# Where softmax is divided: from the probabilities to the output of P @ latents, by a row of reciprocals sent through DRAM

## The chip, the cores and the metric

The kernel runs on one NeuronCore of a Trainium2 chip. A core has TensorE (matrix multiplication, called PE in the profile), VectorE (DVE), ScalarE (ACT), GpSimd (POOL) and SyncE (SP), which here issues all DMAs. The engines run side by side, each through its own list of instructions in order, and wait for each other by semaphores. On-chip data lies in SBUF with 128 partitions; matrix products land in PSUM. The metric is the device time of one execution in microseconds (us); the time of a kernel is the median of several runs.

## What is computed

One pre-norm transformer layer, eight sequences (batches) of 512 tokens, width 512: attention with low-rank queries and a shared latent for keys and values, then a gated feed-forward part with weights rounded to an 8-bit float format. Cut to the attention, where the change lies:

```python
q = rmsnorm(layernorm(x) @ wq_a.T, q_norm_w)                # 384 wide
q_nope, q_pe = split((q @ wq_b.T).reshape(b, s, 16, 192))   # 128 + 64 for each of 16 heads
kv_c, k_pe = split(layernorm(x) @ wkv_a.T)                  # latents 128, rotary key 64
kv_c = rmsnorm(kv_c, kv_norm_w)
k_nope, v = split((kv_c @ wkv_b.T).reshape(b, s, 16, 256))
scores = (q_nope @ k_nope.T + rope(q_pe) @ rope(k_pe).T) / sqrt(192)
attn = softmax(scores, axis=-1)                             # exp(s - max) / sum(exp(s - max))
x = x + (attn @ v).reshape(b, s, 2048) @ wo.T
x = x + ffn(layernorm(x))
```

The kernel folds weights: `wq_b` with the key half of `wkv_b` (tile `wa`), and the value half with `wo` (tile `wst`). Attention then works on the latents themselves: scores are `qn @ latents` plus the rotary part, and the output of a head is P @ latents (128 wide), multiplied by the folded output weights.

## The kernel before

The attention part is a list of 8 x 16 x 4 = 512 steps, one for each batch `b`, head `h` and tile `t` of 128 queries. `at(b, h, t)` is the number of a step. In each step the loop at the end of `attention` first calls `rest` of the step before, then `scores` of this one, and then whatever has been put into `work[i]` for this step, in the order in which it was put. All engines' instructions are recorded in this order (no scheduler moves them), so the position of a call decides where its instruction stands on its engine. In what follows i is the step `at(b, h, 3)` of a head's last tile.

- `scores` (L552): TensorE multiplies one query tile into a PSUM tile `sc` (four passes, L560 and L562). VectorE takes the negative maximum of each row (`nmax`, L564). ScalarE computes `pr` = exp(sc + nmax) with the sum of each row in `den` (L567).
- `rest` inside it (L569), called one step later: VectorE takes the reciprocal of `den` (L571), multiplies `pr` by it (L572), and transposes 32 x 32 blocks of it into `block` (L167, function `blocks`).
- `send` (L172), after every second tile: SP writes `block` (512 KB) to a DRAM tile `way` (L177), and after that has landed reads it back in four parts into `prT`, the transposed probabilities (L179). So transposition goes by way of DRAM.
- `attend` (L577), at step i+6: TensorE multiplies `prT` with the latents `kvt` into the PSUM tile `av` (8 passes, L583), and ScalarE copies `av` into `o`, a tile of the head with queries in the free dimension, and puts the queries back into order in doing so (L586).
- `sums` (L592), at i+7 for odd heads: GpSimd makes sums and differences of the two heads' halves of `o`, for a product by Strassen's method (seven products in place of eight).
- `output` (L606), for every fourth head: seven products of two pairs of heads with `wst` into the PSUM tiles `z_ps`, `u_ps`, `v_ps` (L628), each added to x by VectorE (L632). They are put at i+8 (`z_ps`, `u_ps`), i+12, i+15 and i+16. The odd head of the second pair gives its own `o` to `z_ps`, at step i+8.

`sc`, `av`, `qn_ps` and most other products take turns in one PSUM pool of six buffers (`ps_r`); `u_ps` and `v_ps` have a buffer of their own.

Between these calls lie others, at steps given by hand: projections of queries (`project`, `project_pe`), the latents of the next batch (`put_latents`), and in batches 1 to 6 the rounding of feed-forward weights (`round_piece`, with L71 to L82 on VectorE and L76, L77 on GpSimd). In batch 0 SP also loads the weights of all heads, and they are folded there (`fold_q`, `fold_o`).

`first` prepares the latents of batch 0. Its helper `normed` runs the moments of a tile, the standard deviation (ScalarE), its inverse, and then subtracts the mean.

The feed-forward part follows the attention and is not touched.

Of the kernel before, what the change touches and what calls it, by code (L numbers as in the profile page):

```python
# [35 lines left out]
F32 = mybir.dt.float32  # L36
F32R = mybir.dt.float32r
U32 = mybir.dt.uint32
AF = mybir.ActivationFunctionType
# [47 lines left out]
class Layer:  # L87
# [81 lines left out]
            x.rearrange("p (k c j) -> p k c j", c=NQ, j=Q),  # L169
        )  # L170

    def send(self, out, block):  # L172


        nc = self.nc
        way = self.dram.tile([NQ, Q, NQ, NT * 2 * Q], F32, tag="way", name="way", bufs=6)
        nc.sync.dma_start(way.rearrange("a j c x -> (a j) c x"), block.rearrange("p c k i -> p c (k i)"))  # L177
        for c in range(NQ):
            nc.sync.dma_start(  # L179
                out[c * Q : (c + 1) * Q].rearrange("j a k i -> j a (k i)"),  # L180
                way[:, :, c].rearrange("a j x -> j a x"),
            )

    def ffn_stats(self, x, small):

# [84 lines left out]
    def attention(self):  # L270
        tc, nc, ins, wp, xp = self.tc, self.nc, self.ins, self.wp, self.xp
        with ExitStack() as ctx:
# [279 lines left out]
            def scores(b, h, t, block):  # L552

                qn, qpe = state["qn", b, h], state["pe", b, h // 2]
                lat, _, kpe = state["latents", b]
                q = slice(t * P, (t + 1) * P)
                sc = ps_r.tile([P, S], F32, tag="r", name="sc")
                nc.tensor.matmul(sc, qn[:, q], lat[:, NR, :], start=True, stop=False)  # L560
                for part in range(2):
                    nc.tensor.matmul(sc, qpe[:, h % 2, q], kpe[:, part, :], start=False, stop=part == 1)  # L562
                nmax = sp.tile([P, 1], F32, tag="nmax", name="nmax")
                nc.vector.tensor_reduce(nmax, sc, AX.X, ALU.max, negate=True)  # L564
                pr = hp.tile([P, S], F32, tag="pr", name="pr")
                den = sp.tile([P, 1], F32, tag="den", name="den")
                nc.scalar.activation(pr, sc, AF.Exp, bias=nmax, accum_out=den)  # L567

                def rest():  # L569
                    rden = sp.tile([P, 1], F32, tag="rden", name="rden")  # L570
                    nc.vector.reciprocal(rden, den)  # L571
                    nc.vector.tensor_scalar(pr, pr, rden, None, ALU.mult)  # L572
                    self.blocks(block, pr, t)

                return rest

            def attend(b, h):  # L577
                prT = state.pop(("prT", b, h))
                del state["qn", b, h]
                kvt = state["latents", b][1]  # L580
                av = ps_r.tile([P, S], F32, tag="r", name="av")
                for kt in range(NT):
                    nc.tensor.matmul(av, kvt[:, kt, :], prT[:, :, :, kt, :], start=kt == 0, stop=kt == NT - 1)  # L583
                o = hp.tile([P, S], F32, tag="o", name="o", bufs=6)

                nc.scalar.copy(  # L586
                    o.rearrange("p (u t a i) -> p u t a i", u=2, t=2, i=Q),
                    av.rearrange("p (u a t i) -> p u t a i", u=2, t=2, i=Q),
                )
                state["o", b, h] = o  # L590

            def sums(b, h):  # L592

# [60 lines left out]
            def at(b, h, t=0):  # L654
                return (b * NH + h) * NT + t

            def put(i, f, *args):
                work[i].append(lambda: f(*args))
# [15 lines left out]
            def first():  # L674
                p, state["latents", 0] = latents(0)

                for _ in range(4):
                    pt = ps_r.tile([P, NC, P], F32, tag="r", name="warm")
                    for c in range(NC):
                        nc.tensor.transpose(pt[:, c, :], self.ident, self.ident)  # L680

                def normed(t):
                    p["moments"](t), p["deviation"](slice(t, t + 1)), p["deviation_inverse"](slice(t, t + 1))
                    p["center"](t)

                normed(0)
                p["transpose_x"](0)
                normed(1)
                for t in range(NT):
                    p["project_x"](t, (0,))  # L690
                    if t + 1 < NT:
                        p["transpose_x"](t + 1)
                    if t + 2 < NT:
                        normed(t + 2)
                    p["project_x"](t, (1,))
                p["norms"](), p["norms_inverse"]()
                for t in range(NT):
                    p["scale"](t)
                fold_q(0)
                p["rotary"]()  # L700
                for t in range(NT):
                    p["transpose_l"](t)
                rotate, hi, lo = project_pe(0, 0)
                p["rotary_parts"]()
                rotate()
                fold_q(1)
                project(0, 0)
                hi()
                project(0, 1)
                lo()  # L710
# [12 lines left out]
                    put_q(b, h)  # L723
            for b, h in ((b, h) for b in range(B) for h in range(1, NH, 2)):
                i = at(b, h, 3)
                put(i + 7, sums, b, h)
                if h % G == G - 1:

                    def projected(b=b, g=h // G, i=i):

                        late = (b, g) == (B - 1, NG - 2)
                        when = (8, 12, 17, 18, 19, 20) if late else (8, 12, 15, 16, 16, 18)
                        for n, f in zip(when, output(b, g)):
                            put(i + n, f)

                    put(i + 7, projected)

            for h in range(NH):
                if h >= 2:
# [78 lines left out]
            with tc.manual_schedule():  # L818
                first()
                load_q(2), load_q(3)  # L820
                prT = block = rest = None
                for i in range(len(steps) + 19):
                    if rest:
                        rest()
                        rest = None
                    if i < len(steps):
                        b, h, t = steps[i]
                        if t == 0:
                            prT = state["prT", b, h] = hp.tile(
                                [P, 2, NQ, NT, 2 * Q], F32, tag="prT", name="prT"  # L830
                            )
                        if t % 2 == 0:
                            block = hp.tile([P, NQ, NT, 2 * Q], F32, tag="block", name="block")
                        follow = scores(b, h, t, block)

                        def rest(follow=follow, block=block, prT=prT, t=t):
                            follow()
                            if t % 2:
                                self.send(prT[:, t // 2], block)

                    while work[i]:
                        work[i].pop(0)()
# [125 lines left out]
```

## Time and profile before

| | |
|---|---|
| median of 3 runs | 2741.95 us (2741.65 to 2743.36) |
| the profiled execution | 2745.5 us, of which 2743.7 are the span of the trace |
| TensorE busy | 2718.3 us (99%) |
| VectorE busy | 1884.3 us (69%) |
| ScalarE busy | 895.9 us (33%) |
| GpSimd busy | 597.6 us (22%) |
| DMA | 426 MB, 155 GB/s |

The span runs from the first to the last instruction of one execution. Busy times are sums of the instructions of an engine; a group of the profile is one line of the kernel on one engine with one operation and its tiles, with the count, the busy time, the mean duration of one (ns), and then the idle time of the engine just before, with what ended it. Attention takes the first 2230 us or so, the feed-forward part the rest.

### The profile page before, as it was taken

The page shows a single profiled execution, that of the slowest core. Times are in us where ns is not written, and L with a number is a line of the kernel's source. Part 1 is how long each engine was busy: PE and PEld are TensorE (multiplying, and loading weights), DVE is VectorE, ACT ScalarE, POOL GpSimd, SP SyncE. Part 2 cuts the span into 40 slices and gives each one's busy share as a digit, 9 for nine tenths or more (in the row PEclk, how much of TensorE's full clock was granted, in tenths as well). Part 3 has the DMA queues.
Part 4 walks back from the last instruction along what each step waited for, and adds up shares of the span by engine and source line. Part 5 has one row for each costly group of instructions (what it writes and reads, how often), then busy time and mean ns, then how long its engine had stood idle before and what let it go on. Part 6 is the DMA issues. An engine that isn't in the chain of part 4 may idle for free.

```text
span 2743.7 us, 29211 instructions
## 1 busy us (share of the span) xinstructions
PE 2718.3 (99%) x9280; PEld 1714.8 (62%) x9280; DVE 1884.3 (69%) x3683; ACT 895.9 (33%) x1958; POOL 597.6 (22%) x629
## 2 busy tenths in 40 slices
PE   9999999999999999999999999999999999999999
PEld 5465555555555555555555555555555578888887
DVE  5766787778777877787778777877777734333332
ACT  3333333333333333333333333333332333333332
POOL 1221222222222222122212221222111122222222
PEclk9999999999999999999999999999999999999999
DMA  3654465556555654565456445654565651111110
GB/s 125 207 189 160 167 203 171 157 168 202 169 159 173 201 165 155 171 214 159 154 182 203 159 154 177 208 162 152 183 203 168 201 188 62 66 63 64 66 62 20
DMA packets 262376, 426.07 MB, mean 155 GB/s; under 512 B 29648, under 2 KB 192592, under 8 KB 260688
## 3 DMA queue, kind: packets, MB, share of 16 engines
q1 hardware_dynamic: 262224, 424.21, 47.6%
q8 instruction: 74, 1.21, 0.2%
q14 instruction: 78, 0.64, 0.1%
HBM read 248.99 MB, written 175.11 MB: 155 GB/s over the span
## 4 chain that ended last, share of the span: by engine, by line
PE 90%; DVE 6%; ACT 2%; DMA 1%; issue 0%; SPq 0%; ACTq 0%; DVEq 0%
PE av L583 14%; PE sc L560 14%; PE qn_ps L548 10%; PE u_ps L628 7%; PE sc L562 7%; PE pu L261 6%; PE pd L893 6%; PE pg L261 6%; PE qpe_ps L516 6%; PE lr_ps L451 5%; PE v_ps L628 3%; PE z_ps L628 2%; DVE pr L572 1%; DVE block L167 1%; DVE nmax L564 1%; ACT pr L567 1%
## 5 line engine op out<-in xcount | busy, mean ns | idle before, releaser
L567 ACT ACTIVATE pr<-sc,nmax 128x512 f32<-128x512 f32 x512 | 351.8, 687 | 1294.9 <-DVE nmax L564 1289.1
L562 PE MATMUL sc<-kpe,qpe 128*128 128x512 f32 x1024 | 526.7, 595 | 0.0
L560 PE MATMUL sc<-lat,qn 128*128 128x512 f32 x1024 | 523.1, 592 | 0.0
L583 PE MATMUL av<-prT,kvt 128*128 128x512 f32 x1024 | 462.2, 594 | 3.1 <-DMA prT<-way 2.9
L564 DVE TENSOR_REDUCE nmax<-sc 128x1 f32<-128x512 f32 x512 | 338.5, 661 | 106.9 <-PE sc L562 106.6
L167 DVE STREAM_TRANSPOSE block<-pr 128x512 f32<-128x512 f32 x512 | 364.3, 711 | 27.5 <-DMA way<-block 10.0
L572 DVE TENSOR_SCALAR pr<-pr,rden 128x512 f32<-128x512 f32 x512 | 339.0, 662 | 18.1
L548 PE MATMUL qn_ps<-lat,wa 128*128 128x512 f32 x768 | 350.2, 592 | 0.0
L562 PEld LDWEIGHTS sc<-kpe,qpe 128*128 128x128 f32 x1024 | 194.6, 190 | 244.9 <-issue 242.0
L583 PEld LDWEIGHTS av<-prT,kvt 128*128 128x128 f32 x1024 | 194.3, 190 | 199.9 <-issue 189.0
L416 POOL TENSOR_TENSOR roped<-rope_own,rope_sw 128x512 f32<-128x512 f32 x72 | 91.3, 1268 | 909.4 <-DVE rden L571 822.7
L560 PEld LDWEIGHTS sc<-lat,qn 128*128 128x128 f32 x1024 | 188.8, 190 | 133.1 <-issue 108.8
L548 PEld LDWEIGHTS qn_ps<-lat,wa 128*128 128x128 f32 x768 | 145.2, 189 | 134.6 <-issue 122.6
L881 POOL TENSOR_TENSOR fl<-fuse,fh 128x512 fp32r<-128x512 f32 x96 | 126.1, 1315 | 383.3 <-ACT fh L880 383.3
L877 DVE SCALAR_TENSOR_TENSOR fuse<-pu,us,gate 128x512 f32<-128x512 f32 x96 | 72.0, 750 | 193.9 <-PE pu L261 190.9
L571 DVE RECIPROCAL rden<-den 128x1 f32<-128x1 f32 x512 | 81.3, 159 | 160.6 <-ACT pr L567 153.5
L76 POOL TENSOR_TENSOR q_r<-raw,q_m 128x256 f32<-128x256 f32 x72 | 66.2, 919 | 556.7 <-DVE q_m L74 371.1
L516 PE MATMUL qpe_ps<-lat,wqp 128*128 128x512 f32 x384 | 175.3, 592 | 0.7 <-issue 0.7
L261 PE MATMUL pu<-yh,wu 128*128 128x512 f32 x384 | 149.9, 390 | 0.0
L261 PE MATMUL pg<-yh,wg 128*128 128x512 f32 x384 | 149.7, 390 | 0.0
L893 PE MATMUL pd<-wd,fh 128*128 128x512 f32 x384 | 149.5, 389 | 0.0
L261 PE MATMUL pu<-yl,wu 128*128 128x512 f32 x384 | 149.4, 389 | 0.0
(116 smaller groups left out, 3688.8 us busy)
## 6 DMA issues: line engine op xcount, KB each, us to landing
way<-block SPq DMA_DIRECT2D x256, 512.0 KB, 2.8
prT<-way SPq DMA_DIRECT2D x1024, 128.0 KB, 2.8
wst<-wst_d SPq DMA_DIRECT2D x56, 512.0 KB, 4.4
wst<-wst_d SPq DMA_DIRECT2D x56, 384.0 KB, 3.9
x<-in_hid SPq DMA_DIRECT2D x60, 256.0 KB, 3.5
x<-x SPq DMA_DIRECT2D x16, 512.0 KB, 4.4
out<-o SPq DMA_DIRECT2D x32, 256.0 KB, 2.0
wst_d<-wst SPq DMA_DIRECT2D x8, 896.0 KB, 4.6
```

Source lines behind the costliest of these rows:

```text
L167: self.nc.vector.transpose(out[:, :, :, i : i + Q].rearrange("p c k i -> p k c i"), x.rearrange("p (k c j) -> p k c j", c=NQ, j=Q),)
L261: self.nc.tensor.matmul(ps, self.ffn_w[name, i][:, c * P : (c + 1) * P], y[k][:, c, :], start=c == 0 and k == 0, stop=c == NC - 1 and k == 1,)
L516: nc.tensor.matmul(ps, wqp_s[g][:, r, pj * P : (pj + 1) * P], lat[:, r, :], start=r == 0, stop=r == NR - 1)
L548: nc.tensor.matmul(ps, wa_s[g][:, j, r, :], lat[:, r, :], start=r == 0, stop=r == NR - 1)
L560: nc.tensor.matmul(sc, qn[:, q], lat[:, NR, :], start=True, stop=False)
L562: nc.tensor.matmul(sc, qpe[:, h % 2, q], kpe[:, part, :], start=False, stop=part == 1)
L564: nc.vector.tensor_reduce(nmax, sc, AX.X, ALU.max, negate=True)
L567: nc.scalar.activation(pr, sc, AF.Exp, bias=nmax, accum_out=den)
L572: nc.vector.tensor_scalar(pr, pr, rden, None, ALU.mult)
L583: nc.tensor.matmul(av, kvt[:, kt, :], prT[:, :, :, kt, :], start=kt == 0, stop=kt == NT - 1)
L628: nc.tensor.matmul(got[name][:, t, :], ops[p][left][:, t * P : (t + 1) * P], w[:, p, right, :], start=first and t == 0 and p == 0, stop=la ...
L893: nc.tensor.matmul(pd, f[:, i, t * P : (t + 1) * P], w["wd", i], start=i == 0 and f is fh, stop=i == NI - 1 and f is fl,)
```

## The change

The probabilities stay undivided. `den` becomes a tile of 128 x 4 for a head, and each tile's exp puts its sums into one column. After the last tile, VectorE takes the reciprocal of all four columns at once. P @ latents has the queries in its free dimension, so a divisor is wanted as a row that is the same on all partitions. It is made by two DMAs: one writes the 512 reciprocals to a DRAM tile in order of queries, the other reads them back as a row of 512 onto each of the 128 partitions, with a step of zero for the partition. `send` takes these two calls (`also`): it issues the first between the write to `way` and the four reads, and the second after the reads. `attend` no longer copies `av`; the multiplication of `av` by the row is put at the end of the list of the next step, i+7, on VectorE, in two halves, and writes `o`. `sums` and the call that places the products move from i+7 to i+8; the products stay at i+8 and after. Also, `first` now subtracts the mean before it takes the deviation, and a scratch size of the launch is set to 1024.

```diff
-    def send(self, out, block):
+    def send(self, out, block, also=()):
...
         nc.sync.dma_start(way.rearrange("a j c x -> (a j) c x"), block.rearrange("p c k i -> p c (k i)"))
+        for f in also[:1]:
+            f()
         for c in range(NQ):
             nc.sync.dma_start(
...
             )
+        for f in also[1:]:
+            f()
...
-                den = sp.tile([P, 1], F32, tag="den", name="den")
-                nc.scalar.activation(pr, sc, AF.Exp, bias=nmax, accum_out=den)
+                if t == 0:
+                    state["den", b, h] = sp.tile([P, NT], F32, tag="den", name="den")
+                den = state["den", b, h]
+                nc.scalar.activation(pr, sc, AF.Exp, bias=nmax, accum_out=den[:, t : t + 1])
 
                 def rest():
-                    rden = sp.tile([P, 1], F32, tag="rden", name="rden")
-                    nc.vector.reciprocal(rden, den)
-                    nc.vector.tensor_scalar(pr, pr, rden, None, ALU.mult)
                     self.blocks(block, pr, t)
+                    if t < NT - 1:
+                        return ()
+                    nc.vector.reciprocal(den, den)
+                    way = self.dram.tile([NT, P], F32, tag="den_way", name="den_way", bufs=3)
+                    row = state["den", b, h] = hp.tile([P, S], F32, tag="row", name="row")
+                    source = bass.AP(tensor=way.tensor, offset=way.offset, ap=[[0, P], [1, S]])
+                    return (
+                        lambda: nc.sync.dma_start(way.rearrange("t p -> p t"), den),
+                        lambda: nc.sync.dma_start(row, source),
+                    )
...
-                o = hp.tile([P, S], F32, tag="o", name="o", bufs=6)
-
-                nc.scalar.copy(
-                    o.rearrange("p (u t a i) -> p u t a i", u=2, t=2, i=Q),
-                    av.rearrange("p (u a t i) -> p u t a i", u=2, t=2, i=Q),
-                )
-                state["o", b, h] = o
+                row = state.pop(("den", b, h))
+
+                def normed():
+                    o = state["o", b, h] = hp.tile([P, S], F32, tag="o", name="o", bufs=6)
+
+                    to, by = (v.rearrange("p (u t a i) -> p u t a i", u=2, t=2, i=Q) for v in (o, row))
+                    of = av.rearrange("p (u a t i) -> p u t a i", u=2, t=2, i=Q)
+                    for u in range(2):
+                        nc.vector.tensor_tensor(to[:, u], of[:, u], by[:, u], ALU.mult)
+
+                put(at(b, h, 3) + 7, normed)
...
                 def normed(t):
-                    p["moments"](t), p["deviation"](slice(t, t + 1)), p["deviation_inverse"](slice(t, t + 1))
-                    p["center"](t)
+                    p["moments"](t), p["center"](t)
+                    p["deviation"](slice(t, t + 1)), p["deviation_inverse"](slice(t, t + 1))
...
-                put(i + 7, sums, b, h)
+                put(i + 8, sums, b, h)
...
-                    put(i + 7, projected)
+                    put(i + 8, projected)
...
-                            follow()
+                            also = follow()
                             if t % 2:
-                                self.send(prT[:, t // 2], block)
+                                self.send(prT[:, t // 2], block, also)
...
-    nc = bacc.Bacc("TRN2", target_bir_lowering=False, num_devices=1)
+    nc = bacc.Bacc("TRN2", target_bir_lowering=False, num_devices=1, dynamic_dma_scratch_size=1024)
```

## Prediction

> **What bounds the kernel now.** I read the page first, then the groups of TensorE by form, then the waits, and last the timeline at the places where TensorE stands idle. The page's engine line, its clock row and a VectorE group that goes:
>
> ```profile
> PE 2718.3 (99%) x9280; PEld 1714.8 (62%) x9280; DVE 1884.3 (69%) x3683; ACT 895.9 (33%) x1958; POOL 597.6 (22%) x629
> ...
> PEclk9999999999999999999999999999999999999999
> ...
> L572 DVE TENSOR_SCALAR pr<-pr,rden 128x512 f32<-128x512 f32 x512 | 339.0, 662 | 18.1
> ```
>
> TensorE is busy 99% at full clock, so nothing that another engine does less of is worth its busy time. Only a TensorE idle stretch that goes or comes counts. VectorE is at 69%, off the bound. How much is there to win? Starts of consecutive matmuls in the timeline keep a fixed pace (429 ns for a 512-column float32 pass, 216 for 256 columns). Adding up where a start comes later than that pace gives some 30 us in all: 9 us in the first 100 us, 6 us between 100 and 140 us, and about 2 us in each later batch of 271 us. The groups say who ends the later ones:
>
> ```profile
> L628 PE MATMUL u_ps<-wst,o 128*128 128x256 f32 x512 | 121.8, 381 | 5.9 <-DVE x L632 5.9
> ...
> L628 PE MATMUL z_ps<-wst,o 128*128 128x256 f32 x256 | 62.7, 382 | 5.2 <-ACT o L586 5.2
> ```
>
> After the second bar stands the idle time before: 5.9 us where `u_ps` waits until VectorE has drained it into x (L632), 5.2 us where `z_ps` waits for ScalarE's copy of o (L586). Counted by start to start the L632 wait is 0.95 us in each of batches 1 to 6 (the pair L562 starts at 380.60, the next matmul at 382.43: 1.83 us where 0.88 is usual) and 0.77 us twice in batch 7, 7.2 us in all. The `z_ps` wait is 0.82 us, once a batch.
>
> Now the normal `z_ps`, without a wait (h=3 of batch 1): the timeline of TensorE, then of VectorE (start, length, then engine and line):
>
> ```profile
> 407.24 1.03 PE L562 MATMUL sc<-kpe,qpe 128*128 128x512 f32 x2
> 408.11 1.02 PE L560 MATMUL sc<-lat,qn 128*128 128x512 f32 x2
> 408.57 1.03 PE L562 MATMUL sc<-kpe,qpe 128*128 128x512 f32 x2
> 409.43 1.89 PE L628 MATMUL z_ps<-wst,o 128*128 128x256 f32 x8
> ```
> ```profile
> 410.73 0.65 DVE L564 TENSOR_REDUCE nmax<-sc 128x1 f32<-128x512 f32 x1
> 411.30 0.42 DVE L81 SCALAR_TENSOR_TENSOR q_m<-q_r 128x256 f32<-128x256 f32 x1
> 411.76 0.83 DVE L82 SCALAR_TENSOR_TENSOR done<-q_m,q_r 128x256 fp32r<-128x256 f32 x1
> ```
>
> Call i the step of a head's last query tile. o of head h is made from av at step i+6; `z_ps` is multiplied at step i+8, after the scores of i+7 and i+8. Its first two passes use an older o; from 409.43 + 0.43 = 409.86 it needs the new one. ScalarE had made it at 408.1, 1.7 us early. The maximum of the scores of step i+7 (nmax, 410.73) comes *after* that time on VectorE: VectorE is 2.5 us behind the scores. This order is what the change meets. The one place in a batch where the copy is late (h=11; it runs from 552.21 to 552.78, held up by ScalarE's table loads and casts):
>
> ```profile
> 551.58 0.60 PE L628 MATMUL z_ps<-wst,o 128*128 128x256 f32 x2
> 552.84 1.56 PE L628 MATMUL z_ps<-wst,o 128*128 128x256 f32 x6 [0.66 <-ACT o L586]
> ```
>
> **The change part by part.** *Removed.* 512 reciprocals of 159 ns become 128, 512 multiplications of 662 ns (L572) go, 128 copies L586 of about 0.58 us leave ScalarE. VectorE gets 256 multiplications of 128x256 from PSUM. For these I have L252, the same shape but both operands in SBUF, at 549 ns, L81 (128x256, two float32 inputs) at 420 ns, and L632 with one operand in PSUM at 683 ns for twice the size, with starts 0.60 us apart in a row. I take 0.46 us, 0.36 to the start of the second; ends 0.42 and 0.55. VectorE: -512 x 0.662 - 384 x 0.159 + 256 x 0.46 = -282 us, to about 1600. All of it is hidden under TensorE. Its worth is what it does to the three waits.
>
> *The L632 wait goes.* In that stretch (369 to 382 us) VectorE saves two rows of L571 and three of L572 (0.5 to 1.5 us each), about 3 us; the draining that ended at 382.37 is needed at 381.6. Gain 7.2 us; between 0 and 7.2.
>
> *z_ps waits for VectorE instead of ScalarE.* The multiplication is put at i+7, at the end of that step's list, so on VectorE it stands behind nmax of i+7, and behind L81 and L82 where weights are rounded (batches 1 to 6). It can't start before the scores of i+7 are done: 407.24 + 1.03 = 408.27. With the relief VectorE is there in time. I followed its order from 401 us with the durations shown and the two removed rows left out: it reaches the qpe casts at 405.2, the block of i+6 at 407.0, and waits for the scores. From 408.30: nmax 0.57 to the next start, L81 0.46, L82 0.5 to 0.75, the first multiplication 0.46, and 0.06 to TensorE (as from the copy's end to the release above): 410.35 to 410.60 against 409.86. A new wait of 0.5 to 0.75 us; z_ps reads only the half that the first multiplication writes. Heads 3 and 7 of six batches: 12 x 0.6 = +7.2 us. Where no weights are rounded (h=15, batch 7, batch 0) the same sum without L81 and L82 ends 0.4 us before it is needed: no wait.
>
> At h=11 four more operations (L476, L479 twice, 0.53 us a pair) stand ahead, and ScalarE's chain of 5.51 us from one exp (546.02) to the next (551.53) stays, with its two table loads. It starts earlier by the removed rows: VectorE's block follows L415 at 542.94, nmax 543.8, exp 544.45 instead of 546.02, the next exp 549.96, block 550.7, nmax 551.35, L81 551.9, L82 552.4, L476 to L479 553.2, multiplication 554.25, TensorE at 554.8 instead of 552.84. That is 1.9 us more than the wait that is there, in six batches, and in batch 0, with a further 0.86 us of matmul ahead and no L81, 0.7: +12.1 us. Even with VectorE never late it would be 0.75 us each.
>
> *av keeps its PSUM buffer longer.* It is freed after nmax of i+7. The next user of the slot is a qn two steps later at the nearest; with a projection of 4 us between, it has 4 us to spare. At the other places three or more steps. Nothing. `sums` moves one step; its first reader is four steps on. Nothing.
>
> *Two more DMAs a head on SP.* den goes out (512 elements of 4 bytes) between way and the four prT loads, the row (256 KB) comes in behind them; the row waits on SP for den's landing, with the next head's weights and way queued behind it. In the steady state prT lands some 7 us before its av and SP spends 590 us waiting for VectorE's blocks: hidden. In batch 0 it isn't, since SP also loads weights there; between 60 and 165 us SP waits for a block under 2 us in all. Timelines of SP and TensorE, and a window row (its last three numbers are clock, DMA share, GB/s):
>
> ```profile
> 122.61 0.38 SPq L177 DMA_DIRECT2D way<-block  x1
> 128.60 1.75 SPq L179 DMA_DIRECT2D prT<-way  x4
> ```
> ```profile
> 132.79 5.37 PE L583 MATMUL av<-prT,kvt 128*128 128x512 f32 x8 [2.02 <-DMA prT<-way]
> ```
> ```profile
> 132.60:138.20 5.60, 5.41 (x9) 2.39 (x10) 5.24 (x13) 2.03 (x5) 2.95 (x4) 0.70 0.57 184
> ```
>
> Issue of way, landing 5.6 us later, four issues, landing 2.4 us later, and av starts with it. Slack before av is 4.2 us at head 1, 1.5 at head 2, none at 3 and 4, 6.8 at 5. Each head adds 0.43 us of issue (as the other rows) and 0.7 us of transfer ahead of the next way (at the start the 256 KB x loads, back to back, land 0.66 us apart: the issues at 8.56, 9.22 and 9.88 each wait for a landing); den's issue and landing lie under way's own landing. 1.1 us a head, less 0.5 of slack: head 3 is 2.8 us later, head 4 3.9 in all. The bounds for den: nothing at all, or, since no trace row has 512 packets in one DMA, prT held up behind it. Against this speaks the Trainium skill, DMA: Bandwidth & Descriptors, Rules for kernel authors: a non-contiguous last dimension becomes one descriptor for each element and should be rearranged. Nearest row: knw, 128 packets of 4 bytes, issues in 0.44 us. Four times that is 1.8 us, still under way's landing of 3 to 6 us. By the row +0, by the rule, if each engine's 32 writes take 0.1 us, 3 us a head and 12 in batch 0. I take the row and keep 12 for the range.
>
> The row also shows the clock at 0.70 after the 2.0 us wait: av took 5.37 instead of 3.60 us, 1.8 lost. The Trainium skill (TensorE: Matmul & The Clock Gate, Part 1) asks for a whole idle window of about 3.4 us before the clock halves; this trace did it with 2.0. By the rule a 2.8 us longer wait at head 3 (3.5 us in all) just does it, by the trace surely. +1.7. Batch 0: 3.9 + 1.7 = +5.6 us; between 0 and 17.
>
> *Start.* Centring moves ahead of the deviation, so it no longer waits for ScalarE's table load (1.28 us): xc at 4.5 instead of 6.24, the first transposes at 5.05 instead of 6.77. The weights' landing doesn't hold it (issued by 3.47, 4.9 us to land, the last quarter is needed after 10). -1.7 us; up to -3.4 if the clock also rises one window sooner. *End.* The last head's z_ps needs both multiplications (0.82 us) in place of one copy (0.57): +0.3. The scratch size setting issues nothing: 0.
>
> **Sum.** -7.2 + 7.2 + 12.1 + 5.6 - 1.7 + 0.3 = +16.3 us on the profiled span of 2743.7 (2745.5 with what lies around it). That execution was 3.6 us above the median of the runs; on the median 2741.95 it is 2758.3.
>
> **Rivals.** *The relief is all (faster).* If VectorE had the multiplication done within 1.58 us of the end of scores i+7, neither the old z_ps waits nor new ones are left: -7.2 - 6 x 0.82 - 1.7 = -13.8, 2728 us. For it: VectorE loses 15% of its work. Against it: nmax, L81 and L82 must come to under 1.1 us, and their rows come to 1.5 to 1.8. It decides where the multiplication stands in the order, not how busy VectorE is. *Small waits (no change).* z_ps waits at their least (12 x 0.45, 6 x 0.75), den and clock free, SP 1.2: -1.7 - 7.2 + 5.4 + 4.5 + 1.2 = +2.2, 2744 us. *den is slow.* The scatter holds up the queue by 3 us a head: batch 0 gives 17 instead of 5.6, 2770 us; only above 7 us a head would the later batches follow. That the change doesn't do what it says can't be: TensorE's and GpSimd's orders are the same in both, and the 512 L572 rows are gone.
>
> **How the numbers follow.** Main case 0.66, slow den 0.14, small waits 0.12, relief 0.08. A measurement of this kernel tells about 0.2% (5.5 us) from no change, so slower is 0.66 + 0.14 = 0.80, same 0.12, faster 0.08. The range runs from the small waits (2743) to a slow den with long z_ps waits (2774); outside lie the relief and a little at each end.
>
> **What would show it.** Right: z_ps with an idle time of 20 to 30 us ended by VectorE's o; u_ps<-o without its 5.9; av's wait for prT in batch 0 at 6 us or more; VectorE near 1600 us, ScalarE near 820; xc at 4.5. Wrong: z_ps idle under 8 us, prT landing no later at heads 3 and 4, waits of any other reader for the row, or a qn waiting for o.

## The result, and the profile after

The changed kernel takes 3462.3 us (median of 4 runs, 3459.7 to 3469.7) against 2742.7 beside it: a ratio of 1.2626 (95% interval 1.2603 to 1.2648), +720 us. The prediction was 2758.3 us with a range up to 2774. Slower was right; the size was wrong by a factor of 44.

All lines below are of the changed kernel's trace unless said otherwise; its line numbers are shifted (L597 is the av matmul, L646 the products, L606 the new multiplication, L181 prT's reads, L585 and L586 the writes of den and the read of the row). First the page's engine line and clock row, the av group, and VectorE's transposes, with the idle time before them and what ended it:

```profile
PE 2922.1 (84%) x9280; PEld 1769.2 (51%) x9280; DVE 1529.6 (44%) x3043; ACT 823.3 (24%) x1830; POOL 578.6 (17%) x629
...
PEclk9899999999999989998998899999998898999999
...
L597 PE MATMUL av<-prT,kvt 128*128 128x512 f32 x1024 | 632.0, 775 | 464.7 <-DMA prT<-way 254.5
L167 DVE STREAM_TRANSPOSE block<-pr 128x512 f32<-128x512 f32 x512 | 362.7, 708 | 1348.8 <-DMA way<-block 1291.1
```

The same two groups of the kernel before:

```profile
L583 PE MATMUL av<-prT,kvt 128*128 128x512 f32 x1024 | 462.2, 594 | 3.1 <-DMA prT<-way 2.9
...
L167 DVE STREAM_TRANSPOSE block<-pr 128x512 f32<-128x512 f32 x512 | 364.3, 711 | 27.5 <-DMA way<-block 10.0
```

TensorE is no longer busy 99% but 84%, and its clock row has eights in it (mean granted clock 0.929; 0.999 before). So the loss of 716 us in the span has two parts: 204 us more of busy time (2922.1 - 2718.3) and 513 us more of standing still. Of the 204 us, 170 are av's own passes (775 ns in the mean, 594 before), which run right behind the waits. Nearly all of the standing still is before av (464.7 us, 3.1 before), which waits for prT. The waits view puts 166 of these down to the row, which av doesn't read. In the trace the row landed after av had started in each of those cases, while every one of av's waits ended within 0.45 us of a landing of prT. VectorE's transposes wait 1348.8 us (27.5 before), because their `block` is still being written to `way`. The rows that this stands on are SP's: its DMAs with the median from issue to landing (us), and what SP waited for (total, times, longest):

```profile
way<-block SPq DMA_DIRECT2D x256, 512.0 KB, 6.9
...
den_way<-den SPq DMA_DIRECT2D x128, 2.0 KB, 10.7
```

```profile
SPq L181 <- DMA way<-block: 1766.5, 256, 12.2
...
SPq L586 <- DMA den_way<-den: 154.9, 62, 6.2
...
SPq L177 <- DVE block L167: 13.6, 17, 8.9
```

The same of the kernel before:

```profile
way<-block SPq DMA_DIRECT2D x256, 512.0 KB, 2.8
```

```profile
SPq L179 <- DMA way<-block: 779.6, 256, 5.8
SPq L177 <- DVE block L167: 589.6, 207, 10.5
```

SP's queue is what bounds the kernel now. Before, SP waited 780 us for `way` to land and had 590 us to spare waiting for blocks. After, it waits 1767 for `way` and 155 for den, and the wait for blocks is down to 13.6 us. The sum: 987 more for `way`, 155 for den, 256 more issues at 0.43 us (110), less the 576 of slack used up, is 676 of the 716 us. For a head that is 8.9 us more waiting where 4.6 were spare. One head in SP's timeline (start, length of the issue):

```profile
1004.37 0.38 SPq L177 DMA_DIRECT2D way<-block  x1
1004.84 0.43 SPq L585 DMA_DIRECT2D den_way<-den  x1
1014.33 1.74 SPq L181 DMA_DIRECT2D prT<-way  x4
```

`way` and den are issued at 1004.4 and 1004.8; prT's reads can't go out until `way` has landed, at 1014.3: ten microseconds, where `way` before took 2.6 at this step (9.6 is the median of the 128 such steps now). By the trace's packets, the last pieces of `way` and den are done by 1009.4, and then nothing moves until the landing. A window row (its last three numbers are clock, DMA share, GB/s):

```profile
1009.40:1014.30 4.90, 4.90 (x23) 3.79 (x22) 0.00 (x0) 0.00 (x0) 2.17 (x3) 1.00 0.00 0
```

The DMA engines have nothing left to move; what is late is the completion of the writes.

Last, the groups that the prediction looked at. They answer to the two that were shown of before:

```profile
L646 PE MATMUL u_ps<-wst,o 128*128 128x256 f32 x512 | 124.3, 387 | 4.2 <-DVE x L650 4.2
...
L646 PE MATMUL z_ps<-wst,o 128*128 128x256 f32 x256 | 67.7, 394 | 28.1 <-DVE o L606 27.6
```

`z_ps` waits 28 us for VectorE's multiplication (20 to 30 was forecast), `u_ps` 4.2 instead of 5.9. These were the right places, at 4% of the loss.

### The profile page after: what moved, and what is told of

Same layout as the page of the kernel before. It is cut to its first block, busy times and chain, and to the rows that moved or that the text cites. A ratio compares the mean times of both kernels' runs of the same rounds, so it can differ in the third digit from the quotient of the medians.

```text
span 3460.0 us, 29034 instructions
## 1 busy us (share of the span) xinstructions
PE 2922.1 (84%) x9280; PEld 1769.2 (51%) x9280; DVE 1529.6 (44%) x3043; ACT 823.3 (24%) x1830; POOL 578.6 (17%) x629
## 5 line engine op out<-in xcount | busy, mean ns | idle before, releaser
L597 PE MATMUL av<-prT,kvt 128*128 128x512 f32 x1024 | 632.0, 775 | 464.7 <-DMA prT<-way 254.5
L167 DVE STREAM_TRANSPOSE block<-pr 128x512 f32<-128x512 f32 x512 | 362.7, 708 | 1348.8 <-DMA way<-block 1291.1
L597 PEld LDWEIGHTS av<-prT,kvt 128*128 128x128 f32 x1024 | 246.5, 252 | 796.5 <-issue 697.1
L265 PE MATMUL pg<-yl,wg 128*128 128x512 f32 x384 | 149.4, 389 | 0.0
L911 PE MATMUL pd<-wd,fl 128*128 128x512 f32 x384 | 149.4, 389 | 0.0
```

The lines of the kernel that those rows point to most:

```text
L167: self.nc.vector.transpose(out[:, :, :, i : i + Q].rearrange("p c k i -> p k c i"), x.rearrange("p (k c j) -> p k c j", c=NQ, j=Q),)
L265: self.nc.tensor.matmul(ps, self.ffn_w[name, i][:, c * P : (c + 1) * P], y[k][:, c, :], start=c == 0 and k == 0, stop=c == NC - 1 and k == 1,)
L911: nc.tensor.matmul(pd, f[:, i, t * P : (t + 1) * P], w["wd", i], start=i == 0 and f is fh, stop=i == NI - 1 and f is fl,)
```

## Experiments

Theory A: den's many small writes hold up the landing of what is in the queues with them, and SP waits for that. Rival B: the row does it, 256 KB for each head from one 2 KB line. Rival C: SP's wait for den ahead of the row. The first four runs take the transfers apart.

**Den alone.** The write of den stays; the multiplication takes a constant row.

```diff
-                    row = state["den", b, h] = hp.tile([P, S], F32, tag="row", name="row")
+                    state["den", b, h] = row1          # memset once
-                        lambda: nc.sync.dma_start(row, source),
```

> Left out: the row is not read back (a constant row takes its place); the scatter of the 512 reciprocals to DRAM stays. Theory A, the 512 writes of 4 bytes hold up what is in the queue with them: still slow, 3250 to 3450 us, way landing 6 us or more after its issue. Theory B, 128 partitions reading one 2 KB piece of DRAM are the load: 2750 to 2780 us, way landing at 2.8 us. Theory C, SP standing still before the row until den has landed: 2750 to 2780 us.

3237.3 us, ratio 1.1807 (1.1783 to 1.1830), a little below the forecast range. From its DMA view:

```profile
way<-block SPq DMA_DIRECT2D x256, 512.0 KB, 7.4
...
den_way<-den SPq DMA_DIRECT2D x128, 2.0 KB, 10.3
```

At a head's last step, behind which den is issued, `way` lands after 8.9 us. A holds.

**Row alone.** The row is read from a DRAM tile that was written once; den is not written.

```diff
-                        lambda: nc.sync.dma_start(way.rearrange("t p -> p t"), den),
+                        lambda: None,
```

> Left out: the scatter of the reciprocals (the row is read from a DRAM tile that was written once). Theory A: 2755 to 2780 us, way landing near 3 us. Theory B: 3250 us or more. Theory C: 2755 to 2780 us. If e1 and e2 are both fast, it is C; if both are slow, each transfer costs by itself.

2783.5 us, 1.0152 (1.0132 to 1.0172): B is true, but small.

**Neither transfer.** The constant row, and no DMA; everything on the engines stays as changed.

```diff
-                        lambda: nc.sync.dma_start(way.rearrange("t p -> p t"), den),
-                        lambda: nc.sync.dma_start(row, source),
```

> Left out: both transfers (a constant row). What stays of the change is VectorE's and ScalarE's part and the start. By the steps of the prediction 2753 us (+16.3 less the 5.6 of batch 0 on 2742.65): z_ps waiting 18 to 24 us for o from VectorE, u_ps no longer waiting for x, first xc at 4.5 us. By the rival that the relief is all: 2728 us, z_ps without waits.

2751.3 us, 1.0034 (1.0021 to 1.0047): +9 us. TensorE's wait for the new multiplication (total, times, longest):

```profile
PE z_ps L643 <- DVE o L603: 16.6, 10, 3.9
```

By starts: 0.31 us at heads 3 and 7 of batches 1 to 6, 2.2 us at h=11 of these batches, and 4.4 us in batch 0, at head 3 (the pass that starts at 118.9 and the next). So of the +720: 9 for the engines, 32 for the row, 486 for den (3237.3 - 2751.3), and 193 only where both transfers are there.

**Den in 16-byte pieces.** Each partition writes its four reciprocals as one piece, in order of partitions; the row comes in that order, and VectorE reads it with a stride of four. The same computation.

```diff
-  way = self.dram.tile([NT, P], ...)      dma_start(way.rearrange("t p -> p t"), den)
+  way = self.dram.tile([P, NT], ...)      dma_start(way, den)
...
-  by = row.rearrange("p (u t a i) -> p u t a i", ...)
+  by = row.rearrange("p (a i u t) -> p u t a i", ...)
```

> The same work as the change; the reciprocals go out as 128 pieces of 16 bytes in the order of partitions, the row is read in that order, and VectorE picks its columns in steps of 4 elements. Theory A with a price for each written piece: a quarter of the added 720 us or less, 2800 to 2930 us; if only pieces under some size or neighbours in one line cost, 2755 to 2790. Theories B and C: as slow as the change, 3400 us or more (B), or little better, since den has still to land (C).

2835.5 us, 1.0343 (1.0326 to 1.0360). One layout takes away 627 of the 720 us, with the same bytes to the same stretch of DRAM. The time lies where a price for each written piece was forecast; the runs below show that it isn't the count.

The stride has a price of its own. VectorE's multiplications in the change, and here:

```profile
L606 DVE TENSOR_TENSOR o<-av,row 128x256 f32<-128x256 f32 x256 | 95.5, 414 | 16.9 <-PE av L597 16.9
```

```profile
L607 DVE TENSOR_TENSOR o<-av,row 128x256 f32<-128x256 f32 x256 | 143.9, 603 | 12.5 <-PE av L597 12.5
```

With it `z_ps` waits 43.6 us for them, 26.0 in the run with the row alone. So some 18 of the 52 us by which this run is above that one stand before `z_ps`. Whether the stride makes them isn't shown; no run has it alone.

What is it about the 512 pieces: their number, their size, or that they are neighbours? **Single transfers** at the end of the kernel before:

```diff
+        def case(name, src_shape, dst_shape, to):          # 4 times each
+                nc.vector.memset(s, 1.0)                   # waits for the landing before
+                nc.sync.dma_start(to(d), s)
+        case("a4near", [P, NT], [NT, P], lambda d: d.rearrange("t p -> p t"))
+        case("b4gap64", [P, NT], [NT, P, 16], lambda d: d[:, :, 0].rearrange("t p -> p t"))
...
```

> The kernel before, with single transfers appended at its end, each alone and four times, each waiting for the one before to land: writes of 2 KB to DRAM as 512 elements of 4 bytes in the change's order (neighbours come from different partitions), 512 elements of 4 bytes spaced by 64 and by 512 bytes, 128 of 4, 16, 64, 512 and 4096 bytes, 128 of 16 spaced by 512, 1 of 2 KB, 16 of 128; reads of 256 KB in 128 lines of their own, of one 2 KB line by 128 partitions, of 512 elements of 4 bytes; then a 512 KB write followed at once by the 512 x 4 bytes, and by 128 x 16 bytes. Theory A1 (it is the number of writes to the same stretch of memory: each small write has to wait for the one before it to the same 64 bytes): 512 x 4 near lands after 9 to 11 us also here, spaced by 512 bytes after 2 to 4 us, 128 x 4 near after about 4. A2 (it is the number of small writes, wherever they go): near and spaced alike at 9 to 11 us, 128 x 4 at 3 to 4, 128 x 16 like 128 x 4. A3 (it needs the other traffic: alone they are quick): all below 4 us alone; only the pair is slow. In the pair, A1 and A2 expect the big write's landing put off by 5 to 7 us with the 4-byte writes behind it and by about 2 with those of 16 bytes.

The DMA view of that stretch (KB each, median us to landing; digits at the end of a name are left out by the view):

```profile
dst_m_one2k<-few SPq DMA_DIRECT2D x4, 256.0 KB, 3.4
...
d_a4near<-src_a4near SPq DMA_DIRECT2D x4, 2.0 KB, 9.3
...
d_b4gap<-src_b4gap SPq DMA_DIRECT2D x4, 2.0 KB, 2.1
...
d_e16x<-src_e16x SPq DMA_DIRECT2D x4, 2.0 KB, 1.4
...
dst_n_4x<-few SPq DMA_DIRECT2D x4, 2.0 KB, 2.1
```

512 neighbouring pieces of 4 bytes take 9.3 us with nothing else going on but a second such write beside them (8.8 quite alone, below). The same 512 with 64 bytes from one to the next take 2.1, with 512 bytes 1.8; 128 pieces of 16 bytes take 1.4. *Reading* 512 pieces of 4 bytes takes 2.1, less than a quarter of writing them. 128 neighbours of 4 bytes show no landing in the view, but VectorE could go on only 7.6 to 8.0 us after each issue, so 128 cost nearly what 512 do. So it is neighbours, as in A1, not number. The pairs of a big and a small write came to lie among other cases in time and tell nothing here; the pairs further down do.

**Gaps of 64 bytes, in the kernel.** The run with den alone, each element at 64 bytes from the next.

```diff
-  way = self.dram.tile([NT, P], ...)        dma_start(way.rearrange("t p -> p t"), den)
+  way = self.dram.tile([NT, P, 16], ...)    dma_start(way[:, :, 0].rearrange("t p -> p t"), den)
```

> The run with the den writes alone (3237: 512 writes of 4 bytes in a 2 KB stretch, a constant row in place of the read-back), only that each element goes to 64 bytes of its own. Same count, same sizes, same queue. Theory A1 (neighbouring writes to one 64-byte stretch are done one after the other; alone they landed after 2.1 us in place of 9.3): way's landing back below 4 us, 2752 to 2790. A2 (the number of small writes counts when there is other traffic): 3100 to 3240.

2750.8 us, 1.0030 (1.0018 to 1.0042), where the neighbours gave 3237.3. Landings in its DMA view:

```profile
way<-block SPq DMA_DIRECT2D x256, 512.0 KB, 3.1
...
den_way<-den SPq DMA_DIRECT2D x128, 2.0 KB, 2.8
```

Same number, same size, same queue, 486 us less, and no slower than no write at all (2751.3). That the writes are near each other is what costs; A2 falls. (With the gap the stretch grows too, from 2 KB to 32; the two aren't told apart.)

**How near is near, and whom does it hold?** The same stretch at the end, in a fixed order: gaps alone, then a 512 KB write (`w_`) with the small one (`d_`) behind it on SP, or from ScalarE's queue.

```diff
+        for name, gap in (("a_g4", 1), ("b_g8", 2), ("c_g16", 4), ("d_g32", 8), ("e_g64", 16)):
+            case(name, gap, nc.sync, alone=True)
+        case("f_pg4", 1, nc.sync); case("g_pg64", 16, nc.sync)
+        case("i_actg4", 1, nc.scalar); case("j_actg64", 16, nc.scalar)
...
```

> The kernel before with writes appended at its end in a fixed order. Alone: 512 elements of 4 bytes, 4, 8, 16, 32 and 64 bytes apart. Then a 512 KB write followed at once by the small one: 4 apart, 64 apart, 128 x 16 bytes, each from SP's queue and then from ScalarE's. Alone, 4 apart was 9.3 us and 64 apart 2.1. If writes are held per 64 bytes: 4 to 32 apart fall in proportion (9, 5, 3, 2.5, 2.1). If per 32 bytes: 32 apart is as 64. The big write alone landed after 2.6 us: with 4 apart behind it in its own queue it should land after 7 to 10, with 64 apart or 16 bytes after about 3. From ScalarE's queue: if the hold is the queue's, the big write lands after 2.6 to 3 us; if it is the memory's or the engines', after 7 to 10 too.

The DMA view of this end, with the same columns (the letters are the cases in the diff):

```profile
w_f_pg<-src_b SPq DMA_DIRECT2D x4, 512.0 KB, 2.7
...
w_i_actg<-src_b SPq DMA_DIRECT2D x4, 512.0 KB, 9.5
w_j_actg<-src_b SPq DMA_DIRECT2D x4, 512.0 KB, 2.7
...
d_a_g<-src_s SPq DMA_DIRECT2D x4, 2.0 KB, 8.8
d_b_g<-src_s SPq DMA_DIRECT2D x4, 2.0 KB, 3.1
...
d_e_g<-src_s SPq DMA_DIRECT2D x4, 2.0 KB, 1.9
d_f_pg<-src_s SPq DMA_DIRECT2D x4, 2.0 KB, 9.9
```

Alone, 4 to 64 bytes from start to start give 8.8, 3.1, 2.8, 1.9 and 1.9 us: most of it is gone at 8. That is not in proportion, so A1's picture of one write after the other in each 64 bytes is not confirmed, only that dense ones are slow. Behind a big write on the same queue the big one is not held (2.7; a miss). From ScalarE's queue the small one went out 1.0 to 2.4 us *before* the big one, and the big one landed after 9.5 us in place of 2.7. With 64 bytes between it took 2.7 there, but in those pairs the two went out together, or the small one had landed before. So a big write is held when it is issued while the small writes are not complete, from another queue too.

The two holds look different to the DMA engines. Two window rows of this run: between the last packet of a pair on one queue (2848.4) and the small write's landing at 2855.4, and then while a big write (issued at 2902.55) is held behind a small one from ScalarE's queue (issued at 2901.52):

```profile
2848.50:2855.00 6.50, 0.00 (x0) 0.00 (x0) 0.00 (x0) 0.00 (x0) 0.00 (x0) 0.50 0.00 0
```

```profile
2906.00:2912.00 6.00, 0.00 (x0) 0.00 (x0) 0.00 (x0) 0.00 (x0) 0.00 (x0) 0.50 0.45 16
```

Waiting for the small write alone, the DMA engines do nothing. The held big write has packets open the whole time: of its 128 packets of 4 KB the middle one takes 0.17 us, the longest 7.4, and 16 GB/s move.

In the kernel `way` is ahead of den by 0.47 us and is held all the same. There the packets show den's first pieces going out on some DMA engines while others still have parts of `way` to write (in the run with den alone, 61 pieces of den and 46 of `way` in the half microsecond from 1012.5), which fits; no run isolates this step. There `way`'s packets are done early and its completion is late, as in the window from 1009.4 above.

**Den from ScalarE's queue.**

```diff
-                        lambda: nc.sync.dma_start(way.rearrange("t p -> p t"), den),
+                        lambda: nc.scalar.dma_start(way.rearrange("t p -> p t"), den),
```

> The change, only that the 512 x 4 bytes are issued from ScalarE's queue, not from SP's; the row stays with SP. Theory A as memory (the small writes hold up every write around them): way still lands after 8 us or more at the last step of a head, 3300 to 3500. A as queue (what is held up is the order of SP's own queue): way lands after 3 us, prT's reads go out as before, and only the row is late: 2790 to 2950. Either way ScalarE now waits for VectorE's reciprocal, with an exp behind it.

3531.7 us, 1.2872 (1.2831 to 1.2913), above both forecasts. A, as memory: a queue of its own is no cure. But the place was forecast wrong. Den now goes out later (at 1010.21, `way` of the next head at 1008.13), and it is this next `way` that lands after 10.6 us in the median; the one of a head's last step takes 5.5. TensorE also stands 193 us before `z_ps`, so the time is not `way`'s alone. The run gives the best view of what den's packets themselves take, since that queue (q10) carries nothing else (packets, MB, share of 16 engines' span):

```profile
q10 hardware_dynamic: 67584, 0.27, 1.3%
```

1.3% of 3521 us over 128 heads is 0.36 us a head. The landing is 10.6 us. The DMA share would never have shown it.

**Where the 193 us of both come from.** The change as it is, with the row issued two steps later, behind the next head's first send, so that SP has no wait for den.

```diff
-                        lambda: nc.sync.dma_start(row, source),
+   put(at(b, h, 3) + 3, lambda: nc.sync.dma_start(row, source))
```

> The change as it is, 512 neighbouring writes of 4 bytes, only that the row is issued two steps later, behind the next head's first send. The runs with one part each gave +486 (den alone over neither), +32 (row alone) and +9, of the 720 that the change costs: 190 come only with both. If those 190 are SP's wait for den ahead of the row (155 us in the trace): 3270 to 3320. Rival (the row's read itself is held by the writes and holds the next send): 3400 to 3470.

3375.8 us, 1.2302 (1.2283 to 1.2321): neither number. Taking SP's wait for den away gives back 86 of the 193; the other 106 stay when the row goes out without waiting. That the row's read collides with held writes is likely, but not taken apart further.

**Other repairs.** The reciprocals turned by a 128 x 32 transpose on VectorE, so that each piece has 128 bytes; the row is then read in four pieces of 512 bytes for each partition:

```diff
+                    nc.vector.transpose(den_t, den)
+                        lambda: nc.sync.dma_start(way.rearrange("a (t i) -> (a t) i", i=Q), den_t),
+                        lambda: nc.sync.dma_start(row.rearrange("p (a x) -> p a x", x=P), source),
```

> The change with the reciprocals turned by one 128 x 32 stream transpose on VectorE (its other 28 columns hold ones), written as 128 x 128 bytes, and the row read as four pieces of 512 bytes for each partition. Same computation. Theory A (the small writes hold up what is in the queues with them): the way writes land after 5 us at most, 2783 (the run with the row alone) plus little: 2780 to 2800. Rival (any third write in SP's queue, with a wait for it ahead of the row, costs as much as 128 x 16 bytes did): 2820 to 2850. In both VectorE has 128 more transposes of about 0.1 us.

2892.2 us, 1.0529 (1.0507 to 1.0551): a miss, worse than with 16 bytes. From its DMA view:

```profile
way<-block SPq DMA_DIRECT2D x256, 512.0 KB, 6.0
...
row<-den_way SPq DMA_DIRECT2D x128, 256.0 KB, 6.2
```

The den write is quick (4.1 us), but the row in 512-byte pieces takes 6.2 (4.8 in 2 KB pieces in the run with 16 bytes), and `way` is held up behind it: 7.1 us at a head's second tile against 5.8. I had counted the row as unchanged. Den's part is cured here, and the row's made worse.

**The product a step later.** `z_ps` and the first `u_ps` at i+9, first in the run without transfers:

```diff
-                        when = (8, 12, 17, 18, 19, 20) if late else (8, 12, 15, 16, 16, 18)
+                        when = (9, 12, 17, 18, 19, 20) if late else (9, 12, 15, 16, 16, 18)
```

> The run without either transfer (a constant row: the division is left out of the result), only that the first product of each group is put one step later, at i + 9. Without this it took 2751.3, with 21 us of waits of z_ps for VectorE's o in it (0.31 at heads 3 and 7, 2.2 at h = 11, 4.4 in batch 0). If these waits simply go: 2726 to 2734, below the kernel before: the eviction on VectorE is a gain once the product waits a step longer. Rival: they come back a step later (in the bank that u_ps and v_ps take, or in o's buffers): 2742 to 2752.

2727.3 us, 0.9937 (0.9923 to 0.9952). The waits for the multiplication go and don't come back. The same step in the kernel before, with the centring ahead of the deviation:

> The kernel before, with the centring ahead of the deviation in batch 0, and the first product of each group one step later (i + 9 in place of i + 8). None of the change's division or transfers. In the trace of before, TensorE loses 15.5 us at L628 (to x of L632 and to o of L586) and about 2 us at the start to xc. If a step more of room ends these waits: 2742.7 less 15 to 17.5, that is 2725 to 2729, as good as the constant-row run with the same step (2727), and the eviction's move has nothing left to win. Rival: the product's add on VectorE then lies a step later too and the wait for x or for a bank comes back: 2736 to 2743.

2743.6 us, 1.0005 (0.9997 to 1.0013): no change, a miss. `z_ps`'s waits go there too, but the one for x stays and two new ones come, each once in batches 1 to 6 (TensorE's weight loads: total, times, longest):

```profile
PEld u_ps L628 <- DVE x L632: 10.0, 10, 1.2
PEld lat_pt L486 <- ACT pr L567: 7.4, 6, 1.2
...
PEld qpe_ps L516 <- ACT lat L488: 6.0, 7, 1.0
```

VectorE and ScalarE, still with the 512 multiplications of pr and the 128 copies, are late elsewhere. So moving the division is worth some 18 us (0.9937 against 1.0005), if its row cost nothing and the product had a step more.

**All repairs together:** 16-byte pieces, the row two steps later, the product a step later, the same computation as the change.

> The run with 128 writes of 16 bytes (2835.5, the same computation as the change), and the row issued two steps later, behind the next head's first send, so that SP does not wait for den to land; and the first product of each group one step later. The step later was worth 24 in the runs without transfers. If what is left of 2835.5 is SP's wait for den and the waits of z_ps: 2765 to 2790. Rival (the row's 256 KB for each head and the way it holds up the send behind it are the rest, wherever it is issued): 2795 to 2815.

2777.1 us, 1.0126 (1.0112 to 1.0140). That is 58 below the 16-byte run, and 50 above the one without transfers and with the same step (2727.3).

The row lands in 4.4 us, and `way` in 5.0 (3.4 without transfers). Most of the 50 us lie at the ends. Counted up to the next batch's first `nmax`, batch 0 takes 328 us and batches 1 to 6 together 1624; 824 are left for the rest (318, 1615 and 792 without transfers; 323, 1627 and 794 in the kernel before). In batch 0 SP also loads the weights of all heads, in batch 7 those of the feed-forward part. So the last run has **the change in batches 1 to 6 only**:

```diff
+                if 0 < b < B - 1:   # den, row and multiplication as in the run above
...
+                else:               # reciprocal, multiplication of pr and copy as before
```

> The change with 128 writes of 16 bytes, the row two steps later and the first product of each group a step later (2777) in batches 1 to 6 only; batches 0 and 7 divide on VectorE as before. Same computation. In the trace of that run TensorE loses 64.7 us, of which some 23 in the first 200 us and 33 in the last batch, where weights for the next stage are loaded too, and 8 in between; before loses 30.1, of which 15 in between. If the row's 256 KB is only dear where SP's queue has other loads to carry: 2742 - 7 and some for the two seams: 2733 to 2740. Rival (the row's cost moves with it to the first and last batch that have it): 2745 to 2765.

2739.3 us, 0.9980 (0.9974 to 0.9987; 21 runs): 5.4 us below the kernel before, and the fastest version that computes the whole layer. The three stretches take 319, 1626 and 793 us: the ends are cured, and the middle gains 1 us on the kernel before and 5 on that kernel with the product a step later (1631).

## Why the prediction was wrong

*Two more DMAs a head on SP* is the step that failed, in its words: "den's issue and landing lie under way's own landing" and, of the bounds, "I take the row and keep 12 for the range". The term was +0 for den, 12 at most; alone it measured 486, with the row 679. Three things were wrong with the sizing.

- The row taken, knw with 128 packets of 4 bytes, is a read, and its 0.44 us is the time of the issue. The new operation is a write, and what its readers wait for is its landing. The trace of before had no write of small pieces, so nothing bounded its landing from above; the 12 at the other end was a bound on engine time.
- `way`'s landing was used as cover. But den goes out beside it and moves the cover itself: 2.6 to 9.6 us at that step. A cover has to be a time that the new operation can't change.
- The threshold was passed, and it was too high: "only above 7 us a head would the later batches follow". SP's waiting rose by 8.9 us a head, and they followed, in every batch. But the room that SP had was the 4.6 us a head that it spent waiting for blocks. With den alone it waits 7.5 us a head longer for `way` (1742.5 us in all against 779.6) and issues 0.4 more, and that costs 3.8 us a head (486 over 128 heads), not the 0.9 that a threshold of 7 would leave.

The Trainium skill (DMA: Bandwidth & Descriptors, Rules for kernel authors) had been weighed and put aside. It pointed at the right operation. But the number of pieces is not the price: 512 with 64 bytes between cost nothing here (2750.8 against 2751.3). Nearer to it stands the same page's Anatomy of one DMA — SWDGE (gpsimd) path (here SP issues): most of a DMA's fixed cost of about 2.0 us is the confirmation that the target memory has the last byte, and it can be surprisingly long where that memory is HBM. The idle window above agrees in kind; in size, 2.0 holds here for pieces with gaps (1.9), not for neighbours (8.8).

The clock was a step of its own, "+1.7" at one place in batch 0. What had been read there (0.70 after a wait of 2.0 us) happened behind waits throughout: 204 us of the loss are longer busy time, at a mean granted clock of 0.929.

The other steps can be read in the run without transfers, +9 (5.8 to 12.9) where they sum to 16.3 - 5.6 = +10.7.

- *The L632 wait goes* (-7.2): right there; TensorE no longer waits for x.
- *z_ps waits for VectorE*: the place was right, the size too high at heads 3 and 7 (0.31 for 0.6) and nearly right at h=11 (2.2 for 2.7). At heads 3 and 7, L82 takes 0.34 us to the next start where 0.5 to 0.75 was put, and a multiplication 0.41 in place of 0.46. Batch 0 came out otherwise: 4.4 us at head 3, where no wait was forecast, and none at h=11, where 0.7 was.
- *av keeps its PSUM buffer longer*: nothing, right.
- *Start* (-1.7): the first centring runs at 4.33 instead of 6.24 us, and TensorE's first transposes at 4.87 instead of 6.77. No run has it alone.
- The row's transfer, 0.7 us a head hidden outside batch 0: the row alone is +32. Its half of the step was too small as well.

The rival *den is slow* (0.14) named the mechanism. Its size, 3 us a head, came from 0.1 us for each of an engine's 32 writes, which no row of before showed, and again it was engine time and not landing.

## What to carry to other kernels

Size a DMA by its landing, not by its issue or its engine share, and as a write if it is a write: a transposing store of single elements into one dense line can take 10 us for 2 KB, and it can hold up a write beside it, from another queue too. Give every partition one piece that is contiguous in memory, and undo the order in an access pattern of a compute engine. Count that too: here the stride of four made each multiplication 0.19 us longer. And before calling a new transfer hidden, ask whether the thing that hides it lands as before.

## What the runs showed of the hardware that I had not expected

- Neighbouring 4-byte writes from different partitions: 8.8 us for 512 at 4 bytes from start to start, 3.1 at 8, 1.9 at 32; under 8 for 128 of them; 1.4 for 128 of 16 bytes. Reading 512 such elements: 2.1. What in the memory does it isn't seen.
- While such writes are open, a 512 KB write issued after them from another queue lands after 9.5 instead of 2.7 us, single packets of it taking up to 7.4 us where most take 0.17.
- A VectorE multiplication of 128x256 float32 takes 603 ns with one operand read in a stride of four elements, 414 without.
- 128 partitions reading one 2 KB line take 3.4 us, each its own line 2.6.
